# A two-layer graph attention kernel on one core: gathers released one by one, second-layer scores with the maps as stationary operand, columns of two groups in one product

## The chip, the cores and the metric

The kernel runs on one core of a Trainium2 chip. The metric is the device time of one execution in microseconds; before the change its median is 1094.2 us over 14 runs (1085.7 to 1102.92). A core has five engines with their own instruction streams, each worked through in order: TensorE (PE in the profile; its loads of stationary operands are listed apart as PEld), VectorE (DVE), ScalarE (ACT), GpSimd (POOL) and SyncE (SP). They wait for each other by semaphores, and DMA engines move data beside them. Matrix products write to PSUM, a small memory of eight banks, from which DVE or ACT must copy or use the results before a bank can be written again.

## The reference

Eight graphs share one adjacency matrix of 2048 nodes. A first attention layer has four heads of 64 features and a second layer has one. In a layer the scores of a node are the dot products of its features with those of its neighbours.

```python
def _gat_layer(h, mask, b):
    scores = jnp.einsum('...nd,...md->...nm', h, h)
    scores = jnp.where(mask, scores, NEG)
    attn = jax.nn.softmax(scores, axis=-1)
    return jnp.einsum('...nm,...md->...nd', attn, h) + b
...
mask = graph + jnp.eye(N, dtype=graph.dtype) > 0
h = jnp.einsum('bnc,hdc->bhnd', x, Wh)
out_h = _gat_layer(h, mask[None, None], bh[None, :, None, :])
cat = jnp.transpose(out_h, (0, 2, 1, 3)).reshape(B, N, H * D)
z = jax.nn.leaky_relu(cat, negative_slope=0.2)
h2 = jnp.einsum('bnk,dk->bnd', z, Wo)
out2 = _gat_layer(h2, mask[None], bo)
z2 = jax.nn.leaky_relu(out2, negative_slope=0.2)
...
out = (z2 - mu) * jax.lax.rsqrt(var + LN_EPS) * gamma + beta
...
x = _layernorm(x + _L0_gnn_ref(x, adj, ...), axis=-1)
```

The edge probability falls with the node number: the first nodes have many neighbours, the later ones few.

## The kernel before

The 56 first nodes ("hub rows") are computed against all 2048 nodes. The other 1992 are cut into 166 sets of 12 nodes. For each set the kernel finds, from the adjacency matrix, a list of at most 128 nodes that holds all neighbours of its 12 nodes, and works on that list only: `gather` (L777) fetches the 128 rows, with all eight graphs side by side, from a table in device memory by an indirect DMA that POOL issues (L779). A mask per set says which pairs are edges.

The stages follow each other. The first loads the adjacency matrix, computes the first layer of the hub rows and builds part of the lists. The second, the loop from L959, does the first layer for 83 groups of two sets and builds the rest of the lists. The third does the second layer's hub rows (L1262), the fourth, the loop from L1279, the second layer of the sets in 42 units of four sets. There is no scheduler: the order of the source is the order on every engine, and the two loops are software pipelines written by hand.

In step i of the first layer's loop TensorE does in this order: the last steps towards the second layer's table for groups i-3 and i-2; `scores` of group i+1 (L806); `turn_values` of group i (L848); the transposes of the gathered rows of group i+3 (`turn`, L508); `columns` of group i+3 (L792); `project` of group i (L527); `values` of group i+1 (L831). `columns` multiplies the two sets' own columns, 96 of them, with one 128x128 matrix per head, and ACT's `keep_columns` (L796) stores the result `y`, which `scores` uses two steps later. DVE subtracts the mask from the scores in `weigh` (L811), and ACT takes exponentials in `lift` (L818). POOL runs a one-element memset (L971) on the transposed rows `xTg` that scores have just read, then two gathers for group i+5, and `own_rows` (L786), which copies the own columns of one group.

In iteration u of the second layer's loop TensorE does `scores2` of unit u+1 (L1066), `turn2` of unit u+3 (L508) and `values2` of unit u+1 (L1083). `scores2` has the gathered maps, 128 columns, as stationary operand and 24 columns of a block-diagonal tile `bd` as moving operand, 16 products per unit; the scores come out with the gathered nodes on the partitions. DVE subtracts the mask (L1069) and ACT takes exponentials (L1071). In `values2` the 32 columns of the exponentials `es2` are stationary and four tiles of the array, 32 columns each, work side by side. The outputs of two units share one PSUM tile `op` (tag "O", one buffer). POOL's memset (L1297) on `es2` comes after `values2` of unit u+1, and the four gathers for unit u+5 follow. `turn2` copies the transposed rows with ACT (L1260), two copies per unit.

A pair of units goes through normalization in `norm` (L1096): lists of jobs for eight following iterations, run by `work_on` at the end of an iteration. They divide by the sums (`first`, which also empties `op`), apply the slope (`act`), subtract a mean (`centre`, with a square on ACT), sum the squares (`var`), and scale and add the input (`again`); then the second normalization. Square roots are done for a whole batch at a time, because ACT loads another table for them.

A note for reading: a product of 32-bit numbers appears in the profile as two passes, so 16 products are 32 records; transposes appear once.

## Time and profile before

| what | value |
|---|---|
| median of 14 runs | 1094.2 us |
| the profiled execution | 1097.19 us, span 1095.4 us |
| TensorE busy | 952.9 us, 87% of the span |
| DVE busy | 609.5 us, 56% |
| ACT busy | 558.6 us, 51% |
| POOL busy | 431.0 us, 39% |
| first layer's loop, by its first and last scores | 147.9 to 662.9 us |
| second layer's units, first scores to the end of the last values | 735.9 to 1061.5 us |

The span is the time from the program's first instruction to its last in the profiled execution. Its time beside the span contains the little that lies around it. A line of instruction groups names the source line, the engine, the operation, the output and input tiles, shapes and count, then busy time and mean duration, then the idle time before these instructions with what ended it. The granted clock is the share of full speed at which TensorE ran. In the timeline the first number is the start in us from the span's start, the second the length.

### The profile page before, as it was taken

The page shows a single profiled execution, that of the slowest core. Times are in us where ns is not written, and L with a number is a line of the kernel's source. Part 1 is how long each engine was busy: PE and PEld are TensorE (multiplying, and loading weights), DVE is VectorE, ACT ScalarE, POOL GpSimd, SP SyncE. Part 2 cuts the span into 40 slices and gives each one's busy share as a digit, 9 for nine tenths or more (in the row PEclk, how much of TensorE's full clock was granted, in tenths as well). Part 3 has the DMA queues.
Part 4 walks back from the last instruction along what each step waited for, and adds up shares of the span by engine and source line. Part 5 has one row for each costly group of instructions (what it writes and reads, how often), then busy time and mean ns, then how long its engine had stood idle before and what let it go on. Part 6 is the DMA issues. An engine that isn't in the chain of part 4 may idle for free.

```text
span 1095.4 us, 43054 instructions
## 1 busy us (share of the span) xinstructions
PE 952.9 (87%) x18981; PEld 846.3 (77%) x18981; DVE 609.5 (56%) x1372; ACT 558.6 (51%) x972; POOL 431.0 (39%) x669
## 2 busy tenths in 40 slices
PE   4777786688799999999999995689999999999960
PEld 3554574577788888898988894579999999999960
DVE  3349743489855544555545544213666666676675
ACT  1323442245366556665556662335766666776630
POOL 5542342333344443444443421404545554554300
PEclk9999997799899999999999997887978888898855
DMA  8775522333244344444444422624645656666501
GB/s 185 214 228 147 154 79 76 88 89 89 67 111 108 99 103 108 109 101 106 103 108 110 110 71 83 204 60 118 168 134 161 181 149 163 175 178 168 135 19 26
DMA packets 75538, 133.75 MB, mean 122 GB/s; under 512 B 29519, under 2 KB 45839, under 8 KB 75343
## 3 DMA queue, kind: packets, MB, share of 16 engines
q0 software_dynamic: 26720, 88.55, 30.5%
q1 hardware_dynamic: 31726, 38.17, 12.1%
q10 hardware_dynamic: 16896, 4.20, 2.0%
q8 instruction: 152, 2.49, 0.9%
q14 instruction: 44, 0.35, 0.1%
HBM read 118.15 MB, written 12.71 MB: 119 GB/s over the span
## 4 chain that ended last, share of the span: by engine, by line
PE 71%; DVE 11%; DMA 6%; issue 6%; POOL 3%; ACT 2%; SPq 1%; POOLq 0%; ACTq 0%; DVEq 0%
PE s L1066 15%; PE t L508 15%; PE o L831 7%; PE s L806 7%; PE cat L792 5%; PE o L1083 5%; DMA raw<-in_adj_dram 4%; PE o L848 4%; PE s L865 3%; PE cat L527 3%; DMA gh<-table 2%; POOL a L657 2%; PE s L868 2%; DVE cand L724 1%; PE pk L700 1%
## 5 line engine op out<-in xcount | busy, mean ns | idle before, releaser
L779 POOL DMA_INDIRECT g<-table,index x332 | 325.4, 980 | 127.2 <-issue 111.8
L508 PE MATMUL t<-ident,g 128*128 128x128 f32 x1328 | 198.1, 306 | 2.7 <-issue 2.1
L508 PEld LDWEIGHTS t<-ident,g 128*128 128x128 f32 x1328 | 179.5, 164 | 3.3 <-issue 2.2
L1066 PE MATMUL s<-bd,xTg 128*128 128x24 f32 x1328 | 171.5, 283 | 0.0
L1066 PEld LDWEIGHTS s<-bd,xTg 128*128 128x128 f32 x1328 | 166.8, 207 | 4.2 <-issue 0.7
L855 ACT COPY otb<-o 128x192 f32<-128x192 f32 x166 | 45.0, 322 | 214.7 <-PE o L848 179.5
L838 DVE RECIPROCAL rall<-o 64x8 f32<-64x8 f32 x166 | 34.0, 205 | 143.6 <-PE o L831 142.3
L811 DVE TENSOR_TENSOR e<-s,mask 128x768 f32<-128x768 f32 x82 | 78.4, 956 | 60.1 <-PE s L806 60.1
L831 PE MATMUL o<-g,e 128*64 128x65 f32 x2656 | 95.7, 225 | 10.8 <-ACT e L818 10.8
L831 PEld LDWEIGHTS o<-g,e 128*64 128x64 f32 x2656 | 84.1, 137 | 21.4 <-ACT e L818 13.0
L806 PE MATMUL s<-y,xTg 64*64 64x48 f32 x5248 | 96.7, 223 | 0.9 <-issue 0.9
L806 PEld LDWEIGHTS s<-y,xTg 64*64 64x64 f32 x5248 | 86.1, 137 | 10.2 <-issue 1.0
L1260 ACT COPY xTg<-t 128x1024 f32<-128x1024 f32 x83 | 81.4, 1008 | 22.3 <-PE t L508 22.3
L818 ACT ACTIVATE e<-e,shifts 128x768 f32<-128x768 f32 x83 | 77.7, 937 | 23.3 <-DVE e L811 17.1
L971 POOL MEMSET xTg<- 1x1 f32 x79 | 7.0, 88 | 208.4 <-PE s L806 206.3
L1004 ACT COPY xTg<-t 128x1024 f32<-128x1024 f32 x83 | 82.5, 994 | 6.9 <-PE t L508 6.9
L792 PE MATMUL cat<-xo,gram 128*128 128x96 f32 x640 | 82.6, 272 | 0.0
L792 PEld LDWEIGHTS cat<-xo,gram 128*128 128x128 f32 x640 | 78.0, 192 | 0.0
L1069 DVE TENSOR_TENSOR es<-s,mask 128x384 f32<-128x384 f32 (+1 forms) x42 | 23.2, 553 | 94.4 <-PE s L1066 94.4
L576 ACT ACTIVATE e<-e,shifts 128x896 f32<-128x896 f32 x32 | 33.4, 1042 | 80.2 <-DVE e L573 51.1
L657 POOL TENSOR_SCALAR a<-raw 120x1024 bf16<-120x1024 int32 (+1 forms) x34 | 38.3, 1129 | 76.0 <-DMA raw<-in_adj_dram 47.6
L1071 ACT ACTIVATE es<-es,shifts 128x384 f32<-128x384 f32 (+1 forms) x42 | 25.7, 612 | 78.5 <-DVE var L1093 56.5
(173 smaller groups left out, 1477.7 us busy)
## 6 DMA issues: line engine op xcount, KB each, us to landing
raw<-in_adj_dram SPq DMA_DIRECT2D x32, 480.0 KB
g<-table,index POOLq DMA_INDIRECT x332
table<-x SPq DMA_DIRECT2D x16, 260.0 KB
gh<-table SPq DMA_DIRECT2D x16, 260.0 KB
x<-in_x_dram ACTq DMA_DIRECT2D x32, 128.0 KB
table<-rowt SPq DMA_DIRECT2D x166, 24.4 KB
xr<-in_x_dram SPq DMA_DIRECT2D x164, 24.0 KB
out_dram<-y_s SPq DMA_DIRECT2D x164, 24.0 KB
```

Of the source, the lines that this page charges most:

```text
L508: nc.tensor.transpose(tp[:, q * P:(q + 1) * P], rows[:, q, 1:1 + P], ident)
L657: nc.gpsimd.tensor_scalar(a[:np_, :, m * w:(m + 1) * w], raw[:np_].rearrange("p (c h) -> p h c", h=2), 1.0, 0.0, OP.min, OP.max)
L779: nc.gpsimd.indirect_dma_start(out=t.rearrange("n q c -> n (q c)"), out_offset=None, in_=table, in_offset=bass.IndirectOffsetOnAxis(ap=ind ...
L792: nc.tensor.matmul(cat[:, h // 2, (2 + h % 2) * GM:(3 + h % 2) * GM], gram[:, h, :], xo, start=True, stop=True)
L806: nc.tensor.matmul(sp[half(r), p, (q * 2 + j) * M:(q * 2 + j + 1) * M], xt[half(p), j, q, half(r)], y[half(p), (j * Q + q) * M:(j * Q + q ...
L811: nc.vector.tensor_tensor(e[:, :16 * M].rearrange("p (a q n) -> p a q n", a=2, q=Q), sp[:, :, :8 * M].rearrange("p a (q n) -> p a q n", q= ...
L818: nc.scalar.activation(e[:, :16 * M], e[:, :16 * M], AF.Exp, bias=shifts[:, 0:1], scale=1.0)
L831: nc.tensor.matmul(op[half(p), j, o0:o0 + K1], e[:, c0:c0 + 64], rw[:, q, sums(p)], start=True, stop=True)
L1004: nc.scalar.copy(t, tp)
L1066: nc.tensor.matmul(out[:, :, q, k, :], xt[:, s % 2, q, :], bd[u % 3][:, k, q], start=True, stop=True)
L1083: nc.tensor.matmul(op[t * 32:(t + 1) * 32, f, k * W2 + p:k * W2 + p + K1], e[:, p * Q + q, k, :], rw[:, q, sums(p)], start=(a == 0 and k = ...
L1260: nc.scalar.copy(t, tp)
```

## The change

In the first layer `columns` now takes the own columns of two groups, 192 of them, and does two of the four heads in the step of the even group and the other two in the step of the odd group. `own_rows` copies the columns of two groups in every second step. The number of products per step falls from four to two. The memset on `xTg` is gone. The two gathers of a step are each preceded by `after`, a one-element copy on POOL that reads another engine's result: the first reads ACT's `keep_values` output of group i, the second the exponentials of group i+1. The pool of gathered rows has 11 buffers instead of 12.

In the second layer `scores2` has the tile `bd` as stationary operand, 32 columns per product (12 and 12 used), and the gathered maps as moving operand, 128 columns. The four products of a set, one per pair of graphs, go to the four 32-column tiles of the array, so the scores come out with nodes on the partitions. ACT takes the exponential of all of them straight from PSUM. `turn_scores` then transposes the four sets' exponentials back on TensorE, and DVE multiplies them with a 0/1 mask made by one compare, into `es2`. TensorE's order in iteration u is now `scores2` of u+1, `values2` of u, `turn2` of u+3, `turn_scores` of u+1. The four gathers of iteration u are for unit u+4 and come one after each of: the exponential, the two `xTg` copies of `turn2`, and the masked product, each behind an `after` that reads the named result. In `norm` the odd pairs' jobs are spread over twelve iterations, and square roots are taken every four units. In the hub rows the scores use two single banks, and three units' gathers instead of four are issued ahead.

```diff
-    def own_rows(g):
+    def own_rows(m):
-        t = held["x", g] = work.tile([P, GM], F32, tag="xo", name=f"xo{g}", bufs=3)
+        w = min(4, NS - 4 * m)
+        t = held["x", m] = work.tile([P, 2 * GM], F32, tag="xo", name=f"xo{m}", bufs=2)
...
     def columns(g, cat):
-        xo = held.pop(("x", g))
-        for h in range(H):
-            nc.tensor.matmul(cat[:, h // 2, (2 + h % 2) * GM:(3 + h % 2) * GM], gram[:, h, :], xo, start=True, stop=True)
+        n = min(4, NS - 4 * (g // 2)) * 48
+        for k in range(2):
+            nc.tensor.matmul(cat[:, k, 2 * GM:2 * GM + n], gram[:, g % 2 * 2 + k, :], held["x", g // 2][:, :n], start=True, stop=True)
...
+    spot = const.tile([P, 2], F32, name="spot")
+    def after(ap):
+        nc.gpsimd.tensor_copy(spot[0:1, 0:1], ap)
...
-            if 0 <= i + LOOK < NG:
-                nc.gpsimd.memset(xt[0:1, 0, 0:1], 0.0)
-        if 0 <= i + LOOK < NG and i > -3:
-            for j in range(2):
-                gather(table1, 2 * (i + LOOK) + j, 1, rows_tile)
-        if 0 <= i + 5 < NG:
-            own_rows(i + 5)
         if 0 <= i < NG:
             turn_values(i, op)
             keep_values(i, op)
+        if 0 <= i + LOOK < NG and i > -3:
+            if i >= 0:
+                after(held["ot", i][0:1, H - 1, GM - 1:GM])
+            gather(table1, 2 * (i + LOOK), 1, rows_tile)
         if 0 <= i + 1 < NG:
             lift(i + 1)
+        if 0 <= i + LOOK < NG and i > -3:
+            if i >= 0:
+                after(es[(i + 1) % 2][0:1, 16 * M - 1:16 * M])
+            gather(table1, 2 * (i + LOOK) + 1, 1, rows_tile)
+        if i + 5 < NG and i % 2 and i >= -1:
+            own_rows((i + 5) // 2)
...
-    def scores2(u, sp, e, a):
+    def scores2(u):
...
-                nc.tensor.matmul(out[:, :, q, k, :], xt[:, s % 2, q, :], bd[u % 3][:, k, q], start=True, stop=True)
+                nc.tensor.matmul(sp[q * 32:(q + 1) * 32, k, :], bd[u % 3][:, k, q, :], xt[:, s % 2, q, :], start=True, stop=True,
+                                 tile_position=(0, q * 32))
+        e = held["E", u] = late.tile([P, 4, P], F32, tag="eT", name=f"eT{u}", bufs=2)
+        nc.scalar.activation(e[:, :w], sp[:, :w], AF.Exp, bias=shifts[:, 1:2], scale=1.0)
+        return e[0:1, w - 1, P - 1:P]
+
+    def turn_scores(u, a):
+        w = len(sets[u])
+        e = held.pop(("E", u))
+        te = psum2.tile([P, 4, P], F32, tag="E2", name=f"e2_{u}")
+        for k in range(w):
+            nc.tensor.transpose(te[:, k, :], e[:, k, :], ident)
         m = mask[:, sets[u][0]:sets[u][0] + w, :].rearrange("p s (k h) -> p s k h", h=H)[:, :, :, 0]
-        v = e[:, :, :w, a * SET:(a + 1) * SET]
-        nc.vector.tensor_tensor(v, sp.rearrange("p (b w n) -> p b w n", b=2 * Q, w=4)[:, :, :w],
-                                m.unsqueeze(1).to_broadcast([P, 2 * Q, w, SET]), OP.subtract)
-        nc.scalar.activation(v, v, AF.Exp, bias=shifts[:, 1:2], scale=1.0)
+        on = late.tile([P, 4, SET], F32, tag="on", name=f"on{u}", bufs=2)[:, :w]
+        nc.vector.tensor_scalar(on, m, 0.0, None, OP.is_equal)
+        nc.vector.tensor_tensor(es2[a][:, :, :w, a * SET:(a + 1) * SET], te.rearrange("p k (b n) -> p b k n", n=16)[:, :, :w, :SET],
+                                on.unsqueeze(1).to_broadcast([P, 2 * Q, w, SET]), OP.mult)
+        return es2[a][0:1, 2 * Q - 1, w - 1, a * SET:a * SET + 1]
...
-        return [[first, act, mean(0)], [centre(0)], [var(0)], [again], [mean(1), centre(1)], [], [var(1)], [end]]
+        if v % 2:
+            return [[first, act, mean(0)], [centre(0)], [], [var(0)], [], [], [again], [mean(1), centre(1)], [var(1)], [], [], [end]]
+        return [[first, act, mean(0)], [centre(0)], [var(0)], [again], [], [mean(1), centre(1)], [var(1)], [end]]
...
-    for u in range(-1, NU + 8):
-        a = (u + 1) % 2
+    for u in range(-1, NU + 12):
+        new = list(sets[u + 4]) if u + 4 < NU else []
+
+        def one_more(ap=None):
+            if new:
+                if ap is not None:
+                    after(ap)
+                gather(table2, new.pop(0), 2, rows2)
+
         if u + 1 < NU:
...
-            scores2(u + 1, psum2.tile([P, 2 * Q * 4 * SET], F32, tag="S2", name=f"s2_{u + 1}", bufs=2), es2[a], a)
+            one_more(scores2(u + 1))
+        if 0 <= u < NU:
+            a = u % 2
+            if a == 0:
+                op = bank2(f"o2_{u}", "O")
+            values2(op, sets[u], es2[a], a, len(sets[u + 1]) if a == 0 else 0)
+            if a == 1:
+                spread(u, norm_sets(u // 2, op))
         if u + 3 < NU:
-            turn2(u + 3)
+            turn2(u + 3, (one_more, one_more))
             spread_own(u + 3)
         if u + 1 < NU:
-            if a == 0:
-                op = bank2(f"o2_{u + 1}", "O")
-            values2(op, sets[u + 1], es2[a], a, len(sets[u + 2]) if a == 0 else 0)
-            if a == 1:
-                spread(u, norm_sets((u + 1) // 2, op))
-        if u + 5 < NU:
-            nc.gpsimd.memset(es2[a][0:1, 0, 0, 28:29], 1.0 - a)
-            for s in sets[u + 5]:
-                gather(table2, s, 2, rows2)
+            a = (u + 1) % 2
...
+            one_more(turn_scores(u + 1, a))
+        while new:
+            one_more()
         work_on(u)
```

## The prediction

> **What bounds the kernel now.** I read first, on the page, the TensorE row of the busy tenths beside its granted clock, and then cut the span into stretches.
>
> ```profile
> PE   4777786688799999999999995689999999999960
> ...
> PEclk9999997799899999999999997887978888898855
> ```
>
> ```profile
> 300.00:680.00 380.00, 368.17 (x9156) 328.44 (x9148) 191.71 (x470) 218.01 (x455) 146.05 (x249) 0.99 0.38 98
> 680.00:735.90 55.90, 40.64 (x865) 34.86 (x865) 10.17 (x19) 20.96 (x24) 16.01 (x18) 0.77 0.53 161
> 735.90:1061.50 325.60, 322.39 (x4618) 308.86 (x4616) 204.60 (x389) 207.55 (x303) 153.62 (x188) 0.82 0.54 147
> 1061.50:1095.40 33.90, 0.19 (x2) 0.09 (x2) 20.30 (x46) 4.32 (x9) 0.00 (x0) 0.50 0.13 25
> ```
>
> Columns: length, busy time of PE, PEld, DVE, ACT, POOL, then granted clock, DMA share, GB/s. The stretches are the settled part of the first layer's loop, the second layer's hub rows, the second layer's 42 units, and the tail. TensorE is busy throughout both loops, so it is the bound. But in the units its clock is 0.82 although it never pauses, and 0.77 in the hub stretch, where it pauses. Then one unit, in the timeline:
>
> ```profile
> 850.60 1.95 PE L508 MATMUL t<-ident,g 128*128 128x128 f32 x16
> ...
> 851.91 1.90 ACT L1260 COPY xTg<-t 128x1024 f32<-128x1024 f32 x2
> ...
> 852.48 1.17 PE L1083 MATMUL o<-g,es 128*32 128x65 f32 x64
> ...
> 852.84 0.09 POOL L1297 MEMSET es<- 1x1 f32 x1 [1.53 <-PE o L1083]
> 853.08 1.02 POOL L779 DMA_INDIRECT g<-table,index  x1
> ...
> 853.57 3.75 PE L1066 MATMUL s<-bd,xTg 128*128 128x24 f32 x32
> ```
>
> From L1066 to the next unit's transposes (857.16) this unit takes 6.57 us; the average is 325.6/42 = 7.75. The difference is the half clock: in another unit (866.68 to 876.00, clock 0.64) it is 9.3 us, with the same 16 transposes taking 3.65 instead of 1.95. Last, how long a gather is on its way: GB/s from 402 to 412 us, 40 slices of 0.25 us.
>
> ```profile
> GB/s 120 65 40 19 0 0 0 0 0 0 0 183 166 200 333 183 67 168 116 168 360 230 98 77 46 0 0 0 0 0 0 0 0 100 116 150 283 316 182 133
> ```
>
> Two gathers start on POOL at 403.11 and 404.38; data flow from 404.75 to about 408. The second has landed some 3.6 us after its start. The queues' completion events give a median of 3.8 us (3.4 to 4.5) in the second layer. Now a gather runs two units ahead, so none of this is waited for.
>
> **First layer: columns of two groups at once.** Rows of one step:
>
> ```profile
> 404.41 1.05 PE L792 MATMUL cat<-xo,gram 128*128 128x96 f32 x8
> ...
> 405.38 0.56 PE L527 MATMUL cat<-otb,whT 64*64 64x96 f32 x16
> ...
> 406.77 0.48 ACT L796 COPY y<-cat 128x384 f32<-128x384 f32 x1
> ```
>
> Eight passes of 96 columns go from 404.41 to 405.38: 0.97 us, 0.12 each. After: four passes of 192 columns. L527, with 96 columns and four tiles side by side, needs (0.56 - 0.24 for the last one's own length)/4 = 0.08 us a round, so 192 columns need 0.16: 4 x 0.16 + 0.1 = 0.74. Saved 0.23 a step. Most steps before 300 us take 6.2 to 22 us, not the 5.65 of the steady ones; DVE is 76% busy there (84 of 110 us from 190 to 300), so I credit 65 steps: -15. Against it: scores of an even group now need columns copied in the step just before. ACT ends that copy at 407.25 and scores start at 407.68; 0.2 of the 0.43 margin is left, so +1. POOL's copy of own columns moves the same elements in half as many instructions. **Sum -14**; bounds -19 (all 83 steps) and +14 (the margin missed by 0.5 in 42 steps, the gain kept only in the others). In the first layer POOL's memset (0.09) becomes two copies, waiting for the turned values and the exponentials, so gathers start 1.3 to 1.5 us later in the step. Behind the waits queue own_rows and the early adjacency conversions (1.12 each), all needed a step or more later. Transposes come two steps (11 us) on: cost 0, until a landing exceeds about 8 us.
>
> **Hub stretch.** Twelve gathers are issued ahead instead of sixteen; they share the DMA with the loads of hub rows that TensorE waits for (16.5 us in all at L508). A gather holds all 16 DMA engines for about 1.0 us (queue q0, 30.5% of the span, over 332 gathers), so four less: **-3**, bounds -5 and +2. Scores move to two single banks, halves subtracted separately, same elements: 0.
>
> **Second layer, TensorE's work.** Removed per unit: 3.5 us of L1066 (32 passes at 0.11). Added: 32 passes with 32 stationary and 128 moving columns, four tiles side by side. Nearest row is L1083, 64 such passes of 65 columns in 1.0 us; half as many, twice as long: 1.0. Bounds: 0.9 (eight rounds at a transpose's 0.11) and 3.5 (no overlap). Four transposes at 0.11: 0.5. A unit then holds 1.0 + 1.05 + 1.85 + 0.5 = 4.4 us of TensorE instead of 6.57. I do not take the 2.2 us as gain, because something else is late next.
>
> **The gather loop.** Gathers for unit u+4 are now issued inside iteration u, one after each of: exponential, two xTg copies, masked product; turn2 uses them in iteration u+1. So a ring closes: last eight transposes 1.09, second xTg copy 0.99, POOL copy and gap 0.24, third gather 0.95, copy and gap 0.27, landing of the fourth 3.8 after its start, four hand-overs 0.2: **7.5 us** (7.1 with a landing of 3.4, 8.2 with 4.5). That alone is longer than 6.57. TensorE stands for about 3 us at its second group of transposes. All the rest queues behind: turn_scores, next scores, next values.
>
> **The DVE ring.** The masked product now heads DVE's list and norm work follows. In an odd iteration: product 0.56, older norm's `again` 4 x 0.72, reciprocals and product that empty bank O 1.15, values2 1.17, turn2 1.85, turn_scores 0.5, hand-overs 0.2: 8.3, or 7.5 where two reductions stand in place of `again`. In an even one: 0.56, six or seven DVE passes of 0.69, the last square 0.63 on ACT, the exponential queued behind it 0.65, turn_scores 0.5, hand-overs 0.3: 7.5 to 8.5. The mean of the binding rings is 7.8: 42 x 7.8 = 328 at full clock, against 325.6 now, **+2**. The extra compare (48 columns, about 0.16) runs while DVE waits; 12 square-root batches instead of 24 save ACT time that nobody waits for. Were product and norm work always hidden, 7.5 remains.
>
> **The clock.** The hub stretch shows TensorE with 73% busy, pauses, and clock 0.77, half speed for 46% of the time. After, it is busy 4.4 of 7.8 us with one pause of 3. Half speed follows the pause, thus falls on the ring's own transposes (+1.1) and, in DVE's rings, on 3.5 us of products and transposes. I take +0.72 per unit, about two thirds of a full hit on the short ring: **+30**. Bounds: 0, since the new scores keep the array denser, and +80 (short rings +1.1, long ones +2.7 throughout).
>
> Trainium skill, "TensorE: Matmul & The Clock Gate", section "Why this matters for your kernels": keep pauses between bursts under about 3 us and the clock stays up. Here the units show 0.82 with no pause, so density counts as well, and the measurement decides. By the rule alone a 3 us pause would just pass and the sum would be about 1083; by the row it is the sum below. "TensorEngine Tiling", "Key Properties", says a change of tiling drains TensorE; the order keeps two changes a unit, so it moves nothing.
>
> **Tail.** Odd pairs' norms end eleven iterations after they start instead of seven, so DVE has some 27 passes left at the end, about 18.5 us, against 17 now without the final checks, and three square-root hand-overs: **+4**, bounds 0 and +8.
>
> **Sum.** -14 - 3 + 2 + 30 + 4 = +19. The profiled execution took 1097.19 us (span 1095.4, 1.8 around it), 3 above the median 1094.2 of 14 runs; on the median: **1113**.
>
> **Rivals.** (1) The clock stays up: as above without the +30, 1083, faster. For it: 128-column streams replace 24-column ones; against it: the pause. It decides where the clock in the units is above about 0.92, a third of the lost share and so of the +30. (2) Landing is hidden: the ring does not bind, DVE does with 204.6/42 + 0.16 = 5.0 busy, some 5.7 us a unit with hand-overs: 1094 - 14 - 3 + 4 - 42 x 2.05 = 995; only if a gather landed within 2.0 us, which no row shows. (3) Columns become a wait in the first layer: scores stop 0.3 in half of the steps, +5 there instead of -14: 1132. (4) The four tiles do not run side by side, so the score change does not do what it says: 2.5 us more TensorE per unit, 105 in all, some two thirds of it within the pause: 1150.
>
> **Chances.** Main case 0.59, rival 1 0.21, rival 2 0.04, rival 3 0.10, rival 4 0.06. About 0.5% is what a measurement of this kernel can tell from no change. Main case by itself: 1096 to 1132, 0.07 of it within 0.5%. Faster 0.21 + 0.04 = 0.25, same 0.07, slower 0.68. For 8 in 10 I leave out rivals 2 and 4 and the ends: 1079 to 1136.
>
> **What would show it.** Right: in the units TensorE waits for gathers (none does now), POOL's gathers follow one by one, clock about 0.8, unit 8.5 us; first-layer steps 5.4; L792 four passes at 0.16. Wrong: TensorE busy nearly all of the units, waits ended by DVE or ACT alone, units below 7.6, or steps of 5.65 and more.

## The result, and the profile after

The changed kernel takes 1141.45 us (median of 10 runs, 1137.34 to 1146.93); the kernel before, measured beside it, 1093.7 (47 runs, 1082.18 to 1103.3). The ratio is 1.0467 with a 95% interval of 1.0435 to 1.0499: slower, by 48 us instead of the 19 forecast, and above the range. The profiled execution of the changed kernel took 1136.64 us, its span is 1134.6. One thing is needed to read the numbers below: the result and runs e13 to e18 were measured where the kernel before takes 1092 to 1096 us, runs e1 to e12 where the same kernel takes 1337 to 1359, so what a change is worth is judged only within one of these two groups.

| stretch of the span, us | before | after | difference | forecast |
|---|---|---|---|---|
| start to the first layer's last scores | 662.9 | 648.7 | -14.2 | -14 |
| from there to the first scores of the units | 73.0 | 66.4 | -6.6 | -3 |
| 42 units, to the last values | 324.7 | 375.5 | +50.8 | +32 |
| tail | 34.8 | 44.0 | +9.2 | +4 |
| span | 1095.4 | 1134.6 | +39.2 | +19 |

The rows are those of the two profiled executions; the one of the kernel before lies 3.5 us above its median and that of the changed kernel 4.8 below, so about 8 of the 48 us are not in the table. In the profile of the kernel before, the last values end at 1060.6 us, not at 1061.5 as was read before the change; 0.9 us of the units' 325.6 belong to the tail. "To the last scores" means the start of the last group's scores.

The busy tenths of the changed kernel's page, TensorE and its granted clock:

```profile
PE   5777886687899999999999957867666766675610
...
PEclk9889997799899999999999978897787768786755
```

The same stretches cut out, columns as before (length, PE, PEld, DVE, ACT, POOL, clock, DMA share, GB/s): first layer's settled part, hub rows, units, tail.

```profile
300.00:640.00 340.00, 339.70 (x8572) 295.44 (x8572) 180.78 (x441) 209.99 (x436) 186.48 (x276) 1.00 0.42 109
648.70:715.10 66.40, 43.61 (x1034) 36.31 (x1032) 17.35 (x39) 24.47 (x33) 15.19 (x20) 0.85 0.44 129
715.10:1090.60 375.50, 251.63 (x4784) 208.38 (x4782) 194.67 (x393) 179.95 (x270) 202.38 (x308) 0.78 0.48 128
1090.60:1134.60 44.00, 0.20 (x3) 0.09 (x2) 29.56 (x58) 5.70 (x9) 0.00 (x0) 0.50 0.16 31
```

In the units TensorE was busy 322 of 325 us; now it is busy 252 of 375, and the clock stands at 0.78. Its waits within the units:

```profile
PE t L509 <- DMA g<-table,index: 66.2, 52, 5.2
PE o L1106 <- DVE y_s L1134: 43.4, 19, 3.0
PE e L1088 <- ACT eT L1079: 4.6, 1, 4.6
```

(us in all, times, longest.) Of 124 us without work, 66 are for gathers, as forecast; 43 are for bank O, the PSUM tile of two units' results that DVE has to empty. When each of the two comes shows in the chain of waits through one pair of units. The odd one starts with its scores at 875.64, the even one at 885.33, the next odd one at 895.02:

```profile
875.81 0.56 DVE es L1092
876.36 0.61 DVE y_s L1159
...
877.00 0.70 DVE y_s L1163
...
877.72 0.70 DVE y_s L1164
...
878.45 0.69 DVE y_s L1165
...
879.51 0.70 DVE y_s L1134
...
880.34 1.34 PE o L1106 x64
881.68 3.28 PE t L509 x16
884.97 0.45 PE e L1088 x4
...
887.10 0.98 POOL g L780
888.08 0.18 POOL spot L948
...
888.42 4.66 DMA g<-table,index
...
893.13 1.11 PE t L509 x4
894.24 0.87 PE e L1088 x4
```

The columns are start, length, what. In the odd unit TensorE has finished its scores and stands until 880.34: DVE works through the four passes of an older norm's `again` (L1159 to L1165) before it empties bank O (L1134). By then all rows of the unit have landed, so 16 transposes run in one go. In the even unit bank O is free, but the rows come one by one. POOL in the same pair, from the timeline:

```profile
885.06 0.18 POOL L948 COPY spot<-xTg 1x1 f32<-1x1 f32 x1 [3.29 <-ACT xTg L1289]
885.78 0.97 POOL L780 DMA_INDIRECT g<-table,index  x1 [0.55 <-PE e L1088]
886.76 0.18 POOL L948 COPY spot<-xTg 1x1 f32<-1x1 f32 x1
887.10 0.98 POOL L780 DMA_INDIRECT g<-table,index  x1 [0.16 <-PE o L1106]
888.08 0.18 POOL L948 COPY spot<-es 1x1 f32<-1x1 f32 x1
888.42 0.97 POOL L780 DMA_INDIRECT g<-table,index  x1 [0.16 <-issue]
```

Two xTg copies and the masked product end at 884.6, 886.0 and 886.1, within 1.5 us, because the transposes came in one block. So three gathers are due almost at once, POOL issues them 1.32 us apart, and the last lands 4.66 us after its start. Their data flow without a break from about 887.25 to 893.5, with the norms' loads and stores among them (GB/s from 885 to 895 us, 40 slices of 0.25 us):

```profile
GB/s 0 0 33 66 0 0 0 0 0 83 183 133 116 399 294 136 183 54 158 266 266 311 257 249 216 299 257 235 140 90 82 53 74 41 0 70 37 86 237 33
```

Over 35 units (the sixth to the fortieth) odd units take 8.54 us on average and even ones 10.07. The pair shown is one of two kinds. In nine of the 17 even units DVE runs the passes of an `again` (L1163 to L1165) while POOL issues the second of the three gathers, and that gather then holds POOL for 1.23 to 1.38 us; in the other eight units, as here, it takes 0.97 or 0.98. No run shows the reason.

The first layer's groups: 324 passes in place of 640, their line in the page:

```profile
L794 PE MATMUL cat<-xo,gram 128*128 128x192 f32 (+1 forms) x324 | 65.6, 325 | 0.0
```

### The profile page after: what moved, and what is told of

Same layout as the page of the kernel before. It is cut to its first block, busy times and chain, and to the rows that moved or that the text cites. A ratio compares the mean times of both kernels' runs of the same rounds, so it can differ in the third digit from the quotient of the medians.

```text
span 1134.6 us, 43220 instructions
## 1 busy us (share of the span) xinstructions
PE 865.9 (76%) x18819; PEld 717.6 (63%) x18819; DVE 611.1 (54%) x1390; ACT 533.4 (47%) x941; POOL 523.8 (46%) x823
## 4 chain that ended last, share of the span: by engine, by line
PE 50%; DVE 19%; DMA 14%; issue 6%; POOL 5%; ACT 4%; SPq 1%; ACTq 0%; POOLq 0%; DVEq 0%
PE t L509 11%; DMA g<-table,index 8%; PE o L834 8%; PE s L809 6%; PE cat L794 4%; DMA raw<-in_adj_dram 4%; PE o L851 3%; PE cat L528 3%; PE s L868 3%; PE o L1106 3%; POOL g L780 2%; PE e L1088 2%; DMA gh<-table 2%; DVE var L1155 2%; DVE y_s L1159 2%
## 5 line engine op out<-in xcount | busy, mean ns | idle before, releaser
L780 POOL DMA_INDIRECT g<-table,index x332 | 337.5, 1016 | 107.6 <-issue 45.6
L509 PE MATMUL t<-ident,g 128*128 128x128 f32 x1328 | 211.2, 306 | 77.5 <-DMA g<-table,index 66.2
L509 PEld LDWEIGHTS t<-ident,g 128*128 128x128 f32 x1328 | 168.3, 158 | 100.8 <-DMA g<-table,index 60.4
L948 POOL COPY spot<-otb 1x1 f32<-1x1 f32 x78 | 44.8, 575 | 182.1 <-ACT otb L858 182.1
L1092 DVE TENSOR_TENSOR es<-e,on 128x384 f32<-128x384 f32 (+1 forms) x42 | 23.2, 553 | 179.9 <-PE e L1088 158.2
L1106 PE MATMUL o<-g,es 128*32 128x65 f32 x2656 | 55.1, 244 | 44.2 <-DVE y_s L1134 43.4
L1106 PEld LDWEIGHTS o<-g,es 128*32 128x32 f32 x2656 | 49.8, 125 | 52.4 <-issue 49.6
L794 PE MATMUL cat<-xo,gram 128*128 128x192 f32 (+1 forms) x324 | 65.6, 325 | 0.0
L1150 ACT ACTIVATE sq_s<-y_s 128x512 f32<-128x512 f32 x42 | 26.4, 630 | 79.8 <-DVE y_s L1148 72.0
L515 ACT ACTIVATE z<-cat,bhp 128x192 f32<-128x192 f32 x166 | 61.1, 423 | 1.1 <-PE cat L528 1.1
```

Source lines behind the costliest of these rows:

```text
L509: nc.tensor.transpose(tp[:, q * P:(q + 1) * P], rows[:, q, 1:1 + P], ident)
L515: nc.scalar.activation(z[:, hp], cat[:, :, hp * n:(hp + 1) * n], AF.Identity, bias=bhp[:, hp:hp + 1], scale=1.0)
L780: nc.gpsimd.indirect_dma_start(out=t.rearrange("n q c -> n (q c)"), out_offset=None, in_=table, in_offset=bass.IndirectOffsetOnAxis(ap=ind ...
L794: nc.tensor.matmul(cat[:, k, 2 * GM:2 * GM + n], gram[:, g % 2 * 2 + k, :], held["x", g // 2][:, :n], start=True, stop=True)
L1106: nc.tensor.matmul(op[t * 32:(t + 1) * 32, f, k * W2 + p:k * W2 + p + K1], e[:, 2 * q + p, k, :], rw[:, q, sums(p)], start=(a == 0 and k = ...
```

## The experiments

### The change and the kernel before once more (e13, e15)

Neither is edited.

> The kernel before, unaltered, for its trace on this chip and as a measure of what no change at all shows: ratio 1.00 within 0.01. If the chip is like that of the earlier runs: first-layer stretch about 552 us (515.9 on the first chip), units 12 to 12.5 us (7.75 there) with TensorE's clock below 0.7 in them and pauses at the score passes in which nothing that the trace shows is waited for. If it is like the first chip: 1094 us.

> The changed kernel, unaltered, beside the kernel before and the version with all three waits removed on one chip. Like the earlier chips: ratio 0.92 to 0.94. Like the first: 1.047.

Measured side by side, with the kernel before at 1095.53 us: e13 1091.71, ratio 0.9985 (0.9943 to 1.0027); e15 1144.45, ratio 1.0456 (1.0377 to 1.0535). So the result stands. From the first to the last scores of the first layer the profiles of this pair differ by 12.2 us (515.0 and 502.8), those of the first pair by 16.0. From the last first-layer scores to the first of the units e13 takes 4 us less than the kernel before's first profile and e15 2 us more than the changed kernel's: of the 6.6 us in the table's second row at least half is what two executions of one kernel differ by, and in this pair the two kernels differ by 0.6.

### Single release alone, one unit ahead and two (e7, e14)

e7 gives the kernel before the changed release in the second layer; e14 is the same with gathers for unit u+5 instead of u+4, 24 row buffers instead of 20 and sixteen gathers issued ahead. `one_more` is that of the changed kernel; it is called behind `scores2` and behind each xTg copy, and the rest at the end of an iteration:

```
+            one_more(es2[a][0:1, 2 * Q - 1, len(sets[u + 1]) - 1, a * SET:a * SET + 1])
...
             nc.scalar.copy(t, tp)
+            if then:
+                then(t[0:1, 1, 511:512])
...
-            nc.gpsimd.memset(es2[a][0:1, 0, 0, 28:29], 1.0 - a)
-            for s in sets[u + 5]:
-                gather(table2, s, 2, rows2)
+        while new:
+            one_more()
```

> The kernel before with one part of the change alone: in the second layer the gathers of a unit are issued one by one, each after a one-element POOL copy that waits for a result (scores, two xTg copies), one unit ahead instead of two. Scores, norm order, hub rows and first layer are those before. Theory 'the gather loop is the loss': the ring of 7.5 to 8.2 us, with POOL copies now known to take 0.2 to 0.6 us, is longer than the 6.57 us of TensorE work, TensorE waits for gathers at L508 about 1 us a unit and its clock falls further; units 8.3 to 9 us, total 20 to 50 us above the kernel before. Rival 'the new scores and the longer chain through ACT, TensorE and DVE are the loss': units stay at 7.75, total within 5 us of the kernel before, no waits for gathers.

> The kernel before with its second-layer gathers one by one, each after a one-element POOL copy that waits for scores or an xTg copy, but two units ahead as before the change (24 row buffers), so that nothing waits for a landing. Scores, norms, hub rows and first layer as before. Theory 'four gathers in a row starve TensorE on these chips': with the gathers apart the pauses stay away although TensorE never rests; units 9.5 to 10 us, total 1215 to 1235 where the single release one unit ahead took 1232. Rival 'TensorE's work without a rest is what such a chip slows, by clock and by pauses': with nothing to wait for it is busy throughout again, units above 11.5 us, total above 1300. On a chip like the first: 1094 within 10 us by both.

e14: 1100.22 us, ratio 1.0024 (0.9973 to 1.0074). From the first to the last scores of the units 319.4 us, against 322.2 and 321.0 in the two profiles of before, and no wait for a gather. Releasing gathers one by one, with a POOL copy for each, costs nothing as long as they run two units ahead. e7 ran where the kernel before takes 1337 us and took 1231.96 there (0.9195, 0.9156 to 0.9234); it was expected above, not below. TensorE waits for gathers there 5.3 us in all, where about 1 us a unit was expected. From the first to the last scores its units last 412 us where those of an unchanged second layer last 509 (e6, below), at a clock of 0.71 against 0.68. What makes the old units so slow there is not settled: e14 was meant to tell and met the other condition.

### Gathers off the loop (e17 and e9; e2 and e8)

e17 and e9 are one kernel, the changed one without the copies that hold gathers back:

```
         def one_more(ap=None):
             if new:
-                if ap is not None:
-                    after(ap)
                 gather(table2, new.pop(0), 2, rows2)
```

> Gathers of the second layer released by their row buffers alone, all else as changed. Where the kernel before takes 1095: TensorE waits 66 us in the changed kernel's units for gathers, nearly all in even units (10.0 us each, odd ones 8.5 to 8.8). If bank O and the gathers are in series, even units fall to 6.5 to 7.5 and odd ones stay: 21 x 2.5 to 3.5, so 50 to 75 us off 1144, ratio 0.98 to 1.00. If bank O then takes the time instead, even units fall but odd ones grow by as much: less than 25 us off, ratio above 1.02. Where the kernel before takes 1340: ratio 0.90 to 0.91 as before.

> The changed kernel without the one-element POOL copies of the second layer: a gather is released by its row buffer alone (20 buffers, so by the transposes four units back), no longer by the exponentials, xTg copies and masked products of the unit in work. All else as changed. In the trace of the changed kernel TensorE stands 66 us of the 375 us of units at transposes for gathers, and three gathers released together start 1.3 us apart and land up to 4.7 us after their start. Theory 'the gather loop makes the even unit long': those waits go, as with the gathers two units ahead, and the total falls by some 28 to 40 us against the changed kernel (1245 on the chips of the earlier runs, 1141 on the first). Rival 'releasing them singly is what pays, whatever the loop': the gathers bunch again, TensorE pauses and the total stays within 10 us of the changed kernel or rises.

e17: 1073.94 us beside 1091.62, ratio 0.9887 (0.9792 to 0.9983), that is 70 us below e15, or 62 by the two ratios. Its units last 307 us where those of e15 last 380 and those of the first profile 375. One edit turns the loss into a gain of about 1%, just clear of none by its interval. TensorE's waits in its units:

```profile
PE o L1106 <- DVE y_s L1134: 48.7, 20, 3.6
PE e L1088 <- ACT eT L1079: 42.3, 18, 4.3
```

None for gathers. Even units take 6.94 us instead of 10.07, odd ones 8.46 instead of 8.54: the gathers were the even unit's wait and that alone. A new wait stands in the even unit, for the exponentials, which ACT has queued behind the norm's squares. e9, the same kernel in the other condition, takes 1234.67 (0.906, 0.8989 to 0.913); from the first to the last scores its units last 350.7 us, those of the changed kernel in that condition 382.8 (e5).

The same by another way: the gathers stay chained, but run two units ahead.

```
-        new = list(sets[u + 4]) if u + 4 < NU else []
+        new = list(sets[u + 5]) if u + 5 < NU else []
```

(and 24 row buffers, sixteen gathers issued ahead.)

> The changed kernel with the gathers of the second layer issued for unit u+5 instead of u+4 (24 row buffers, one unit more ahead at the start); every release stays. Theory A (the gather ring is the main cost): TensorE's 66 us of waiting for gathers at the transposes go, unit 8.94 to about 8.0 us, time 1141 - 35 = 1105. Theory B (DVE's ring through bank O and the squares in front of the exponential bind as tightly): waits move to DVE and ACT, unit above 8.6, time 1125 to 1141.

> The changed kernel with its second-layer gathers two units ahead again (24 row buffers instead of 20, sixteen gathers ahead instead of twelve), still released one by one; all else as changed. Theory 'the gather loop is the loss': waits for gathers at L509 go, units fall from 8.94 to about 7.6 us, which the rings through bank O and DVE then set (7.5 to 8.3 at full clock), total about 1141 - 42 x 1.3 = 1086. Rival 'bank O, the squares and DVE set the unit, gathers only come last by a little': units stay above 8.5, total above 1122.

1216.2 (0.9109, 0.9036 to 0.9182) and 1216.68 (0.9078, 0.9027 to 0.9129), against 1245.01 for the changed kernel (e5). In e8 even units fall from 9.31 to 7.02 us, odd ones stay (9.66 and 9.83).

### Bank O emptied first (e18, e10)

```
         for k, part in enumerate(parts):
+            if k == 0:
+                jobs.setdefault(u, []).insert(0, part[0])
+                part = part[1:]
             jobs.setdefault(u + k, []).extend(part)
```

> Bank O emptied ahead of the other norm jobs, all else as changed. Where the kernel before takes 1095: TensorE waits 45 us for bank O in odd units. In series: odd units start their products 2 to 2.8 us earlier, the transposes and gathers behind them too, so 21 x 1.5 to 2.8, 30 to 55 us off 1144, ratio 0.995 to 1.02. If gathers alone set the pair: within 8 us of the changed kernel, ratio 1.04 to 1.05. Where the kernel before takes 1340: ratio 0.90 to 0.91 as before.

> The changed kernel with one thing moved: the three DVE instructions that empty bank O (two reciprocals, one product) stand in front of an iteration's other norm jobs instead of behind the four passes of the older norm's 'again' (4 x 0.70). In the trace of the changed kernel every odd unit holds TensorE at values2 for them until 3.7 or 4.7 us after the unit's start, 43 us in all. Theory 'the pair of units is one ring, bank O and then the late transposes' gathers, in series': values2 starts about 2 to 2.8 us earlier in odd units, its transposes and copies too, so the next unit's gathers as well: 21 x 1 to 2.8 us, 20 to 55 us off the total. Rival 'gathers alone set the pair': the wait at values2 is replaced by one for gathers of the same length, total within 8 us of the changed kernel.

e18: 1114.56 us, ratio 1.0263 (1.017 to 1.0356), 30 us below e15, or 21 by the two ratios: the lower end of what the series theory gave, or less. Its waits in the units:

```profile
PE t L509 <- DMA g<-table,index: 88.0, 73, 3.4
...
PE o L1106 <- DVE y_s L1134: 5.2, 7, 0.8
```

Bank O's 43 us are gone, but 22 us more are spent on gathers. Products start 1.92 us into the odd unit instead of 4.07, and the transposes behind them now meet rows that have not landed: their stretch grows from 2.37 to 3.88 us. Odd units take 7.95, even ones 8.96: the even unit gains 1.1 us although only the odd unit's wait was removed, which fits that wait being what brings the releases together. A pair is 1.7 us shorter, part of it by the clock (0.84 in the units instead of 0.78). So bank O's wait counts, but much of what it leaves is filled by waiting for gathers: in this kernel the loop of the gathers is the longer one. e10, the same kernel in the other condition: 1229.53 (0.9014, 0.8944 to 0.9085).

### The norms' schedule (e11)

```
-        if v % 2:
-            return [[first, act, mean(0)], [centre(0)], [], [var(0)], [], [], [again], [mean(1), centre(1)], [var(1)], [], [], [end]]
...
-        at = [2 * v + 1 + (4 if v % 2 else 2), 2 * v + 1 + (8 if v % 2 else 6)]
+        at = [2 * v + 3, 2 * v + 7]
```

> The changed kernel with every norm again spread over eight iterations as before the change, instead of twelve for odd pairs (24 square-root batches instead of 12). Theory 'the tail is longer because odd norms end later': the stretch after the last unit falls from 44 to about 37 us, DVE's time in it from 29.6 to about 22, and the units change by less than 10 us (twelve more square-root table loads of 1.3 us on ACT, beside a wait that is there anyway). Rival 'the tail is DVE's whatever the schedule': still 43 to 45 us.

1237.96 us (0.9085, 0.9015 to 0.9157). Units and tail of e11, and then of the unedited kernel in the same condition (e5):

```profile
819.60:1196.50 376.90, 258.37 (x4784) 212.31 (x4782) 201.82 (x418) 209.03 (x299) 193.87 (x308) 0.86 0.49 128
1196.50:1234.50 38.00, 0.44 (x14) 0.09 (x3) 27.61 (x57) 6.34 (x11) 0.00 (x0) 0.50 0.16 31
```

```profile
818.00:1207.60 389.60, 262.61 (x4786) 217.47 (x4782) 194.44 (x393) 180.32 (x270) 203.11 (x308) 0.82 0.46 123
1207.60:1251.70 44.10, 0.28 (x10) 0.09 (x2) 29.88 (x58) 5.70 (x9) 0.00 (x0) 0.54 0.16 31
```

The tail loses 6.1 us, as expected, so the longer schedule is most of the 9 us by which the tail had grown. DVE has nearly as much left to do (27.6 against 29.9), so what goes is mostly waiting between its steps. The units lose 13 us too, a little more than was thought possible: an odd unit's products start at 3.30 us on average instead of 4.07.

### Order on ACT, and all of it together (e3; e12 and e16)

e3 is e2 with bank O emptied first and an iteration's norm work issued behind the next scores, so that exponentials stand ahead of squares; e12 and e16 are one kernel: that order, gathers free as in e9, norms as in e11.

```
         if u + 1 < NU:
             one_more(scores2(u + 1))
+        work_on(u - 1)
...
         while new:
             one_more()
-        work_on(u)
+    work_on(NU + 11)
```

> As the run with gathers two units ahead, and in addition the pair's first job (which empties bank O) stands first among an iteration's norm jobs, and an iteration's norm jobs are issued after the next unit's scores and exponential, so that squares no longer stand in front of the exponential on ACT. If rings through gathers, bank O and squares are together the cost, what remains is DVE's own work of 5.0 us and POOL's four gathers of 1.3 us: unit 5.6 to 6.3 us, time 1141 - 42 x 2.9 = about 1020. If the score form itself or the half clock is the cost, the unit stays above 7.5 us and the time above 1080.

> The three edits together, and an exponential put ahead of the squares in ACT's list (norm work of an iteration issued behind the next unit's scores): gathers released by buffers alone, bank O emptied first, norms in eight iterations. Every cause that I name for the units is out. Theory: nothing waits for gathers or for bank O, a unit then is TensorE's 4.4 us at its granted clock plus the hand-over scores, exponential, turning, masked product: 6.5 to 7.5 us, total 60 to 90 us below the changed kernel, below the kernel before on any chip (1050 to 1085 where that takes 1094). Rival 'the clock, not the waits, sets the units': TensorE at half speed through most of them, units above 8 us, total less than 40 us below the changed kernel.

> The version of the changed kernel with gathers released by buffers alone, bank O emptied first, norms in eight iterations and exponentials ahead of squares, again, now beside the changed kernel. Like the earlier chips: ratio 0.87 to 0.88 to the kernel before, about 0.94 to the changed kernel, that is 70 us below it: 37 from the gathers, 26 from bank O, 12 from the norms, as each took off the units alone. If the three overlapped instead of adding (a rival that the single runs do not exclude, since they were on two chips), 40 us or less. On a chip like the first: 1050 to 1085.

e3: 1204.63 (0.9023, 0.8951 to 0.9095). Its units take 8.1 us on average (340/42), not the 5.6 to 6.3 of the theory; beside 19 us for bank O, TensorE stands 58 us before the values there with nothing to wait for that the profile shows. e12: 1188.92 (0.8719, 0.865 to 0.8787). e16, beside e13 to e15: **1013.19 us**, 0.9272 of the kernel before (0.9201 to 0.9342) and 0.885 of the changed kernel (1013.19/1144.45): it beats both. Page and units:

```profile
PE   4786687678789999999999999856887777777720
...
PEclk9989999769989999999999999957999989899865
```

```profile
719.60:970.70 251.10, 199.84 (x4786) 179.19 (x4782) 201.55 (x418) 203.17 (x299) 146.21 (x146) 0.91 0.67 184
```

Units last 251 us against 375 and 325; TensorE's work in them, 252 us in the changed kernel, is 200, with the clock at 0.91 instead of 0.78. Even units take 4.55 us on average, and 4.25 in the 11 of 17 where TensorE waits for nothing, which is its work at full clock. Odd ones take 7.73, still with a wait for bank O: 20 waits, 46.5 us in all, no less than the 43.4 of the changed kernel (the profile puts them down to a DVE memset that follows L1134). So this run does not take bank O's wait away. An odd unit whose scores start at 850.08 shows where it comes from:

```profile
850.51 0.69 DVE L1165 TENSOR_TENSOR y_s<-y_s,xr 128x512 f32<-128x512 f32 x1
851.12 0.68 DVE L1148 SCALAR_TENSOR_TENSOR y_s<-st_s,y_s 128x512 f32<-128x512 f32 x1
...
852.01 0.56 DVE L1092 TENSOR_TENSOR es<-e,on 128x384 f32<-128x384 f32 x1
...
852.49 0.41 DVE L1132 RECIPROCAL rall<-o 64x8 f32<-64x8 f32 x2
852.93 0.69 DVE L1134 TENSOR_TENSOR y_s<-o,rall 128x512 f32<-128x512 f32 x1
...
853.77 1.19 PE L1106 MATMUL o<-g,es 128*32 128x65 f32 x64 [2.61 <-DVE var L1116]
```

The instructions that empty the bank (L1132, L1134) head their iteration's norm work, but DVE still has the iteration before in hand: an older `again`, a `centre` and the masked product. What went is the waiting for gathers, as in e17, and the waiting for exponentials, 42.3 us in e17 and 3.1 here. Together the edits bring 131 us. Free gathers alone account for about 70 of them (e17). The other 60 are spread over the exponentials put ahead of the squares, the clock (TensorE's work in the units is 15 us less than in e17) and the norms in eight iterations (the tail is 6 us shorter than in e17); no run takes the order on ACT alone. DVE and ACT, 202 and 203 us busy in the 251, are now as full as TensorE.

### TensorE kept busy (e4), and the first layer alone (e1, e6; e5)

e4 puts products nobody uses into the changed kernel, ahead of the second group's transposes:

```
             tp = bank2(f"t2_{g}", "T", 2)
+            for k in range(6 if g % 2 else 0):
+                nc.tensor.matmul(tp[:, 0, :200], ident, own[:, k * 200:k * 200 + 200], start=True, stop=True)
```

> The changed kernel with six extra products (128 x 128 by 200 columns, about 0.33 us each at full clock) in front of the second group of transposes of each unit, where TensorE waits for gathers; their results are overwritten. If half speed after the pause is a cost of its own (0.72 us per unit predicted), the clock in the units rises from 0.78 to above 0.93 and the unit falls from 8.94 to about 8.2 us, time about 1110. If the clock does not matter beside the rings, the time stays at 1141 or grows by up to 42 x 1 us.

1264.12 us (0.9461, 0.9386 to 0.9537), against 1245.01 for the changed kernel there: 19 slower. From the first to the last scores of the units the clock went from 0.83 to 0.93 and waits for gathers fell from 36 to 14 us, yet this stretch lasted 398 us instead of 383. The filler is itself 98 us of TensorE time in line with the rest. It shows that denser work brings the clock up, not that this pays.

e1 and e6 are one kernel: the first layer's edits alone, the second layer as before.

> The kernel before with the first layer's part of the change alone (columns of two groups in one product, gathers released singly, 11 row buffers); second layer as before. If the first layer gained what the two profiles show (last scores at 648.7 instead of 662.9 us), the time is 1094 - 14 to - 16 = 1079, ratio 0.986, steps 5.44 instead of 5.65 us. If the gain came only because later stages absorbed a delay, the ratio is 1.00. The units then stay at 7.75 us.

> Only the first layer's part of the change (columns of two groups in one pass, gathers released one by one there); the second layer is the one before the change. Theory 'the first layer is worth -14, the loss is all in the second': first-layer stretch 14 us shorter, total 14 us below the kernel before (1080 beside 1094), units at 7.75 us. Rival 'the first layer's later gathers cost as much as its passes save': total within 4 us of the kernel before. On a chip that pauses as the one of the earlier runs did, the stretch should still be no longer than that of the kernel before.

> The changed kernel itself, unaltered, so that it stands on the same chip as the three kernels run with it. If this chip behaves like the one on which the change was timed, 1141 us beside 1094 for the kernel before (ratio 1.047). If it behaves like the one on which the kernel before took 1338 us, where TensorE pauses about 0.56 us once a step for nothing that the trace shows and the clock falls to 0.68 in the old units, both theories expect the change to look better than it is: the old units hold 6.57 us of TensorE work each, the new ones about 4.4, so a slower TensorE costs the old ones more; then 1230 to 1280, ratio below 0.97.

e1 1362.25 (1.0194, 1.0076 to 1.0312), e6 1364.7 (1.0148, 1.0066 to 1.023): 1.5 to 1.9% slower there, where the theory had a gain. From the first to the last scores the first layer takes 576 us in e6 and 552 in e7, whose first layer is the one before. In the other condition it takes 515.0 (e13) and 502.8 (e15). The gain of the first layer thus does not hold everywhere; the first layer's edits alone were not timed in the condition of the result. e5: the changed kernel takes 1245.01 there, 0.9281 of the kernel before (0.9232 to 0.933): the sign of the whole change turns. What TensorE waits for in e6's units:

```profile
PE s L1075 <- issue: 37.7, 98, 0.9
PE o L1092 <- issue: 19.4, 58, 0.5
```

These are pauses with nothing visible to wait for, and the clock in these units is 0.68. The old units, dense with TensorE work, suffer most: 510 us from first to last scores where they take 321 in e13, while the changed kernel's take 383 (e5) and 373 (e15).

## Why the prediction was right or wrong

**Direction and mechanisms: right.** What it said would show is there: TensorE waits for gathers in the units (66 us; none before), POOL issues one by one, the clock is 0.78, first-layer steps are 5.44 us, L794 takes four passes 0.16 us apart. e14 and e17 show the main one: on the old units the release costs nothing while no landing is waited for, and opening the loop gives the changed kernel 62 to 70 us back.

**First layer, -14: right** in the condition of the result: -14.2 (-12.2 in the loop of the second pair), and the steady steps fall from 5.65 to 5.44 us, 0.21 where 0.23 was estimated. Rival 3 (columns become a wait) is out there.

**Hub stretch, -3:** -6.6, beyond the bound of -5; but e13 shows 4 us between two executions of one kernel, and the second pair differs by next to nothing. Nor is the reason shown: TensorE's waits for the hub rows fall from 16.5 to 7.8 us, but one of 7.0 us for DVE comes up in their place. Not settled more finely.

**TensorE's new work: right.** 32 score passes take 1.08 us at full clock (estimated 1.0), so four tiles run side by side and rival 4 is out. All of a unit's work takes the 4.25 us of those even units of e16 that wait for nothing; the sum had 4.4.

**Second-layer rings, 7.8 us a unit: the failed step, by the size of its gather term.** Its odd units, 8.3 or 7.5, were to take 7.9 + 0.72 = 8.6 us on average with the clock, and take 8.54 (9.3 with an `again` in front of bank O and 7.8 without, for 9.0 and 8.2): the DVE ring is right. For a mean of 7.8 the even ones were to take 7.7 + 0.72 = 8.4, and take 10.07. The even iteration's DVE ring was added up wrongly besides: its terms, 0.56, six or seven passes of 0.69, 0.63, 0.65, 0.5 and 0.3, make 6.8 to 7.5, not 7.5 to 8.5, so the gather ring of 7.5 was the longer one there and the mean was 7.7; this errs the other way, by about 4 us. The term "second xTg copy 0.99, POOL copy and gap 0.24, third gather 0.95, copy and gap 0.27, landing of the fourth 3.8" lets POOL be free when the second copy ends, and takes the median landing. In the pair shown POOL still has the gather of the first copy in hand until 886.75, 0.75 us after the second copy ended, and the last of the three gathers lands after 4.66 us. Over 16 even units (a 17th, of 13.57 us, is left out) the next gather starts 1.29 us after the second copy ends, instead of 0.24; the last one starts 1.79 us after that, instead of 1.22; and it lands after 4.14 us (3.67 to 4.80), instead of 3.8. From the end of the copy to the landing that is 7.2 us in place of 5.3. The prediction had one ring or the other binding; it did not see that the odd unit's wait gathers up the releases for the even unit. e17 shows the term: with the gathers free, even units lose 3.1 us and odd ones none.

**The clock, +30: right in kind, somewhat small.** From the first products to its end the odd unit takes 8.54 - 4.07 = 4.47 us; at clock 1.00 (e16, even units without a wait) the same work takes 4.25 - 0.90 = 3.35. In the even unit the last transposes and the turning back take 1.11 and 0.99 instead of 0.65 and 0.55. That is 1.1 + 0.9 a pair, 42 us over 42 units: an estimate from these rows, for TensorE's time on the ring alone. Of 1.57 us a pair that the steady units are above the forecast, it makes about 0.6; the rest is the gather term, of which some is hidden behind the odd unit's wait. Rival 1 is out: in the changed kernel the clock is 0.78, and it needed 0.92. The Trainium skill's rule ("TensorE: Matmul & The Clock Gate", "Why this matters for your kernels"), that pauses of up to about 3 us keep the clock, is not what the traces show: e16's odd units, with one pause each of 2.3 us on average and none over 2.7 in the 18 steady ones, stand at 0.88, 11 of them at 0.79 or 0.80 and seven, four with pauses of 2.6 or 2.7, at 1.00; its even units, whose waits are 0.5 us at most, stand at 1.00.

**Tail, +4:** +9.2, 1 beyond its bound. The count of DVE passes fell short: DVE is busy 29.6 us there against 21.2 before, 8.4 more, where the sum had 18.5 against 17. e11 takes 6.1 of the tail away by the schedule.

**Rival 2** (units of 5.7 us by DVE, 995 us) was given 0.04 because no gather lands within 2 us. So it is; but units nearly as short come with the loop opened instead: 251/42 = 6.0 in e16.

Not foreseen at all was that the sign depends on the condition: e5 stands at 0.928 where e15 stands at 1.046.

## What to carry to other kernels

When gathers are released by results of the work in hand, follow the ring round both units of a pair: a wait in one unit bunches the releases, and they then stand in line on the issuing engine in the next. Give a chained transfer one stage more of lead than its landing needs, or let free buffers alone release it; free buffers were worth 62 to 70 us here, and in the condition of the result nothing was gained by holding gathers back (e14, e17). In the other condition e7 was 8% faster with them held back, and why is not settled. And when an engine loses 2 us of work a unit, look at once for what is late next, queue by queue: bank O behind an older norm, exponentials behind squares. Free gathers alone brought 70 us and bank O alone 30; all edits together brought 131, although the wait for bank O came back in e16, because DVE had other work in front of it. So look at the waits again after each edit: one that was removed alone can return when the engine behind it becomes the fullest.

## What the runs showed of the hardware beside this

- A one-element POOL copy took 0.18 us as a rule, but 0.575 on average in the first layer's loop (78 copies, 44.8 us) and 0.379 after the masked products (38 copies); the estimate had 0.24 with its gap, from a memset of 0.09.
- The condition of e1 to e12: the kernel before takes 1337 to 1359 us there. With the same granted clock of 1.00 between 400 and 500 us, TensorE pauses in e2 once a step in the eight passes of L868, 6.4 us in all in these 100 us, some 16 steps; they run without a pause in the changed kernel's first profile; in dense second-layer units the clock is 0.68 besides. Gather landings in the first layer's loop are as elsewhere (median 3.6 to 3.7 us, from the queues' completion events). The record gives the chip number 2 for e5 to e8 as well as for e13 to e16, so the condition does not go by that number. No run shows the cause.
